# A two-layer cross-attention transformer on one core: the first cross group prepared eight groups ahead, extra rounds of maxima moved behind the second round of scores, constant rows written by DMA, and adjacent chunks for two copies

## The chip, the core and the metric

The kernel runs on one core of one Trainium2 chip. The time is device microseconds of one execution. Before the change three runs took 3248.24, 3252.8 and 3247.61 us; the median is 3248.24 us. Five engines work beside each other: TensorE (PE, with its weight loads PEld), VectorE (DVE), ScalarE (ACT), GpSimd (POOL) and SyncE (SP), which here only issues DMAs. Each engine runs its own instructions in the order in which the program has them, and waits on semaphores for the others.

## What is computed

Two layers, each with self attention, cross attention and a gated feed-forward, over 4 batches of 512 tokens with 320 features. Everything is float32. There are 20 heads of 16 features; self attention has 512 keys, cross attention 1601 keys from a context with 192 features.

```python
h1 = ln(x, n1_g, n1_b);  x = attn(h1, h1,      q1, k1, v1, o1_w, o1_b) + x
h2 = ln(x, n2_g, n2_b);  x = attn(h2, context, q2, k2, v2, o2_w, o2_b) + x
h3 = ln(x, n3_g, n3_b)
a, g = split(h3 @ ff_w1 + ff_b1);  x = (a * gelu(g)) @ ff_w2 + ff_b2 + x

def attn(x, ctx, wq, wk, wv, wo, bo):      # 20 heads of 16
    s = softmax((x @ wq) . (ctx @ wk) * 16 ** -0.5)   # over all keys
    return (s . (ctx @ wv)) @ wo + bo
```

## The kernel before, in words

**Groups.** Attention is cut into groups of 4 heads of one batch (`Unit`). A layer has 20 self groups (4 batches x 5 groups), then 20 cross groups, then 4 feed-forward units. I number the attention groups through: 0 to 19 are self groups of layer 0, 20 to 39 its cross groups, 40 to 59 the self groups of layer 1, 60 to 79 its cross groups. Group 20 and group 60 are the first cross group of a layer; the code calls them `early`.

**Maxima first.** The softmax subtracts a row's maximum inside the matmul: queries and keys lie in slots of 32 rows of which 16 are features and one is the negated maximum (in q) against a row of ones (in k). So before a group's scores can be made, its raw scores must be computed once in the other orientation (`max_pairs`, matmuls at L880 and L904 into PSUM tiles `sps`), reduced by VectorE (L896, L916), turned, and written into q by eight small DMAs on SP's queue (`max_end`, L951).

**Chunks and rounds.** `main` (L1042) walks over chunks of 128 keys: 4 chunks in a self group, 13 in a cross group. A chunk has two rounds. A round is two score matmuls (L1051, tiles `st`) and beside them, in the other half of TensorE's rows, a pair of maxima matmuls for a later group. ScalarE takes the exponential of each score tile into a `pr` tile (L1057). After the second round `flush` issues the product with the values of the chunk before (L1071, `av`); ScalarE copies it to a tile `vo` (L1087) and GpSimd adds that to the sum `o` (L1088). `pr` and `vo` share a ring of 8 buffers. Then `steps` takes work from queues (`chains`), each piece with a cost and a due round: projections of queries (L676), keys (L702, L732) and values (L807, L825), output projections (L998), transposed norms (L478).

**Extra rounds.** A self group's own rounds have room for exactly the maxima of the next self group (8 pairs), and a cross group's 26 rounds for the 26 pairs of the next cross group. The first cross group of a layer has no cross group in front of it, so its maxima need rounds of their own: four maxima matmuls at a time, two in one double PSUM tile (`ps_m`, 2 tiles of 2 banks) and two in single banks (`ps_st`, a ring of 4 that also holds scores, values and projections). `giver` decides when such a round is owed; in `main` it runs after `steps`, at L1112 to L1115, which means directly in front of the next chunk's two rounds.

**Preparing ahead.** While group i runs, the main loop (L1353) adds the projections of group i + 3, or of group i + 5 if that is `early`; `lead`, `add_norms` and `giver` have distances that go with it (4, 6 and 5 groups).

**Constant rows.** The key buffers `kbuf[1]` and `kbuf[2]` of cross attention hold ones and zeros outside of the features. `rows_of_ones` (L129) writes them on GpSimd: a memset and two passes over 64 partitions for each buffer of 128x1664. In layer 0 this is on a list `loads`, from which `main` takes one entry after each chunk; in layer 1 it follows the last feed-forward unit of layer 0, which uses the same buffers.

**Context keys and values.** Four 128-wide quarters go to four banks: two singles, which ScalarE copies out, and a double tile, which VectorE copies out (`quarter_banks`, L740 to L742, L832 to L837).

Of the kernel before, what the change touches and what calls it, by code (L numbers as in the profile page):

```python
# [22 lines left out]
P = 128  # L23
# [19 lines left out]
HALF = QT // 2  # L43
NHC = FF // P

PARTS = [(0, 2 * HG), (2 * HG, H)]
# [19 lines left out]
def kernel(ctx: ExitStack, tc: tile.TileContext, x, context, ws, out):  # L66
# [61 lines left out]

    def rows_of_ones(k, new=True):  # L129

        if new:
            nc.gpsimd.memset(k, 0.0)
        for b in range(2):
            rows = slice(b * GD, (b + 1) * GD)
            nc.gpsimd.tensor_scalar(k[rows], k[rows], zero[rows], ones[b][rows], ALU.mult, ALU.add)

# [6 lines left out]
    zero = const.tile([P, 1], F32, name="zero")  # L143
    nc.vector.memset(zero, 0.0)


# [449 lines left out]
    def lead(u):  # L596

        if u.i == 0:
            return 0
        return units[u.i - (4 if u.early else 2 if u.m == 0 else 1)].start  # L600

# [24 lines left out]
    def add_proj(u):  # L626
# [97 lines left out]
        def keys_of_context():  # L724
# [15 lines left out]
            for i, ps in enumerate(singles):  # L740
                nc.scalar.copy(stage[:, 2 * i, :], ps[:, : HALF + 32])
            nc.vector.tensor_copy(stage[:, 1::2, :], both[:, :, : HALF + 32])  # L742

# [42 lines left out]
    def quarter_banks(name):  # L786

        both = ps_m.tile([P, 2, 512], F32, tag="m", name=name)
        singles = [ps_st.tile([P, 512], F32, tag="st", name=name) for _ in range(2)]
        return [singles[0], both[:, 0], singles[1], both[:, 1]], singles, both  # L790

    def add_values(u):
# [24 lines left out]
        def values_of_context(i, s):  # L817
# [14 lines left out]
            for a, ps in enumerate(singles):  # L832
                nc.scalar.copy(vals[:, 4 * s + 2 * a, h0:h1, 0:DH], ps[:, :w].rearrange("p (h d) -> p h d", d=DH))
            nc.vector.tensor_copy(
                vals[:, 4 * s + 1 : 4 * s + 4 : 2, h0:h1, 0:DH],
                both[:, :, :w].rearrange("p a (h d) -> p a h d", d=DH),
# [205 lines left out]
    def main(u, give, nxt):  # L1042
# [49 lines left out]
        for c in range(u.nch):  # L1092
            extra = []
            if last:

                both = ps_m.tile([P, 2, N], F32, tag="m", name="st")
                round_of([lambda j=j: score(c, j, both[:, j % 2] if j > 1 else None) for j in range(HG)], [])
                tick()
            else:
                for odd in range(2):  # L1100
                    if odd:
                        tick()
                    pair, rounds = give(2 * c + odd)
                    extra += rounds
                    round_of([lambda j=j: score(c, j) for j in ((2, 3) if odd else (0, 1))], pair)
            u.scored = c + 1
            flush()
            late.append(lambda c=c: values(c))
            steps(None, 1 if extra or c == u.nch - 1 else 2)

            start["both"] = True
            for i, e in enumerate(extra):  # L1112
                if i and next_cost() is not None:
                    run(pick())
                round_of([], e)  # L1115
            start["both"] = False
            if not last and c == u.nch - 3:
                max_reduce(nxt)
                max_end(nxt)
            if loads:  # L1120
                loads.popleft()()
# [7 lines left out]
    def add_norms(i):  # L1129

        while norms and norms[0].i <= i + (1 if norms[0].kind == "ff" else 6):
            u = norms.popleft()
# [86 lines left out]

    EARLY = 9  # L1220

# [13 lines left out]
    def after(u):  # L1235

        stage[u.b] += 1
        if u.b == B - 1:
# [5 lines left out]
            if u.l + 1 < L:  # L1244
                if u.kind == "ff":
                    for k in kbuf[1:]:
                        rows_of_ones(k, False)
                    loads.extend(load_cross(u.l + 1))
# [17 lines left out]
    def giver(u):  # L1266

        ahead = []  # L1270
        for v in units[u.i + 1 : u.i + 6]:
            if v.kind == "ff":
                break
            if v.i <= u.i + 2 and (v.i == u.i + 1 or u.kind != "ff") or v.early:
                ahead.append(v)
# [5 lines left out]
        def give(h, alone=False):  # L1281
# [5 lines left out]
            most = 0.0  # L1287
            for v in ahead:
                total += left(v)
# [3 lines left out]
                if rest > 0:  # L1293
                    most = max(most, (total - rest * (not alone)) / (2 * rest))
                if left(v) and (rest == 1 or alone and rest < 1):
                    owed = max(owed, 1.0 if alone and rest > -4 else (left(v) + 1) // 2)
            owed += most * went if total else 0.0
            while owed >= 1.0 and any(left(v) for v in ahead) and not (alone and rounds and rest > -4):
                hand = [v for v in ahead if left(v) and all(v.pairs) and at_hand(v)]
                if not hand and ahead[0].start - 4 - clock["round"] > 1:  # L1300
                    break
                v = hand[0] if hand else next(v for v in ahead if left(v))
                at_once(v)
                rounds.append([f for q in v.pairs if q for f in q.popleft()])
# [34 lines left out]
    now(load_x(1))  # L1339
    rows_of_ones(kbuf[0][:, 4 * QT :])  # L1340
    loads.extend(load_x(2))
    for k in kbuf[1:]:
        loads.append(lambda k=k: rows_of_ones(k))
    for fs in (load_out(0, "o1_w"), load_x(3), load_cross(0), load_ff(0)):
# [8 lines left out]
    for i, u in enumerate(units):  # L1353
# [9 lines left out]
        start["both"] = u.kind == "ff"  # L1363
        for k in (3, 5):
            v = units[i + k] if i + k < len(units) else None
            if v is not None and v.kind != "ff" and v.early == (k == 5):
                add_proj(v)
# [30 lines left out]
```

## Time and profile before

| what | value |
|---|---|
| runs | 3248.24, 3252.8, 3247.61 us |
| profiled execution | 3249.95 us |
| its span, first to last instruction | 3248.2 us |
| TensorE clock granted, mean | 0.996 |
| DVE busy | 2061.2 us (63%) |
| ACT busy | 1969.5 us (61%) |
| POOL busy | 1217.6 us (37%) |
| self attention of layer 0 (scores of groups 0 to 19) | 33.8 to 429.7 us |
| cross attention and feed-forward of layer 0 | 429.7 to 1657.5 us |
| self attention of layer 1 | 1657.5 to 2045.4 us |
| cross attention and feed-forward of layer 1 | 2045.4 us to the end |

Busy shares say little here: four matmuls of 32 rows run beside each other, and a wait of 1 us between two rounds vanishes in a share of 98%. What can be read is the distance between the starts of successive rounds on TensorE, in the timeline: two rounds of one chunk stand 0.98 us apart, the second round and the `av` behind it 0.95 us, `av` takes 0.88 or 1.00 us. Where a distance is larger, TensorE waited, and the timeline's bracket behind an instruction names the wait. Every matmul of the program appears twice in the counts, as two passes.

### The profile page before, as it was taken

What the parts mean: (1) busy time and instruction counts of PE and PEld (TensorE: products, weight loads), DVE (VectorE), ACT (ScalarE), POOL (GpSimd) and SP (SyncE); (2) the same over time, 40 slices, a digit from 0 to 9 for tenths busy, and PEclk for the clock granted to TensorE, in tenths of its full rate; (3) what the DMA queues carried; (4) which work ended last, traced back from release to release, by engine and by line L of the source; (5) the groups of instructions that cost most, each with busy time, mean ns of one, the idle gap of its engine ahead of it and who ended that gap; (6) DMA issues with size and microseconds to landing.
All of it is one profiled execution on the core that took longest, in us unless ns stands there. A gap on an engine that the chain in (4) does not pass through costs nothing.

```text
span 3248.2 us, 81861 instructions
## 1 busy us (share of the span) xinstructions
PE 3197.9 (98%) x33970; PEld 1481.1 (46%) x33970; DVE 2061.2 (63%) x2663; ACT 1969.5 (61%) x3951; POOL 1217.6 (37%) x1627
## 2 busy tenths in 40 slices
PE   8999999999999999999999999999999999999999
PEld 3444444444444444354444444444444444443555
DVE  6777777777777777422247777777777777773221
ACT  3666567777777777611136665677778777775110
POOL 5545334434444443210234544344434444432000
PEclk9999999999999999999999999999999999999999
DMA  1121011100100100100002100010010010001000
GB/s 52 43 53 33 16 25 36 38 21 19 33 21 19 32 16 10 39 6 1 1 22 48 31 12 16 20 30 16 16 29 12 16 32 10 16 10 37 9 10 15
DMA packets 98008, 74.46 MB, mean 23 GB/s; under 512 B 42717, under 2 KB 88165, under 8 KB 97637
## 3 DMA queue, kind: packets, MB, share of 16 engines
q1 hardware_dynamic: 97552, 69.22, 8.8%
q8 instruction: 268, 4.39, 0.6%
q14 instruction: 104, 0.84, 0.1%
q0 software_dynamic: 64, 0.00, 0.0%
q10 hardware_dynamic: 20, 0.00, 0.0%
HBM read 33.04 MB, written 7.93 MB: 13 GB/s over the span
## 4 chain that ended last, share of the span: by engine, by line
PE 93%; DVE 2%; POOL 2%; issue 1%; ACT 1%; DMA 0%; SPq 0%; POOLq 0%; DVEq 0%
PE st L1051 25%; PE av L1071 20%; PE sps L880 14%; PE fps L1167 9%; PE yps L1206 5%; PE ops L998 3%; PE kps L732 3%; PE qps L676 3%; PE vps L825 3%; PE fps L1179 2%; PE vps L807 2%; PE sps L904 1%; PE kps L702 1%; PE hps L478 1%; DVE pm L896 1%
## 5 line engine op out<-in xcount | busy, mean ns | idle before, releaser
L1057 ACT ACTIVATE pr<-st 128x512 f32<-128x512 f32 (+1 forms) x2720 | 1414.4, 602 | 488.1 <-PE sps L880 343.0
L1051 PE MATMUL st<-q,kT 32*128 32x512 f32 (+1 forms) x5440 | 1382.9, 617 | 33.5 <-ACT pr L1057 12.9
L896 DVE TENSOR_REDUCE pm<-sps 128x2 f32<-128x1024 f32 (+1 forms) x970 | 1136.1, 1206 | 273.1 <-PE sps L880 265.5
L880 PE MATMUL sps<-kT,q 32*128 32x512 f32 x5120 | 1285.0, 623 | 2.3 <-DVE nmax L896 2.0
L1088 POOL TENSOR_TENSOR o<-o,vo 128x512 f32<-128x512 f32 x576 | 735.6, 1277 | 1392.1 <-ACT vo L1087 1220.0
L1051 PEld LDWEIGHTS st<-q,kT 32*128 32x128 f32 (+1 forms) x5440 | 516.0, 181 | 559.8 <-ACT pr L1057 313.2
L1071 PE MATMUL av<-pr,vals 128*32 128x512 f32 (+1 forms) x5440 | 732.7, 607 | 0.2
L896 DVE TENSOR_REDUCE nmax<-sps 128x2 f32<-128x1024 f32 (+1 forms) x343 | 378.8, 1145 | 156.7 <-PE sps L880 153.5
L880 PEld LDWEIGHTS sps<-kT,q 32*128 32x128 f32 x5120 | 408.6, 184 | 108.4 <-issue 87.0
L1087 ACT COPY vo<-av 128x512 f32<-128x512 f32 x576 | 348.0, 604 | 41.5 <-PE av L1071 38.7
L1071 PEld LDWEIGHTS av<-pr,vals 128*32 128x32 f32 (+1 forms) x5440 | 110.0, 108 | 498.5 <-ACT pr L1057 473.3
L1167 PE MATMUL fps<-hT,w 128*128 128x512 f32 x640 | 288.2, 599 | 1.1 <-DVE hid L1186 0.6
L1185 ACT ACTIVATE gl<-fps,b 128x512 f32<-128x512 f32 x80 | 50.6, 684 | 387.4 <-PE fps L1179 387.4
L624 POOL TENSOR_SCALAR q<-qst,keep,zero 64x128 f32<-64x128 f32 (+1 forms) x476 | 229.9, 483 | 49.7 <-ACT qst L688 16.7
L1167 PEld LDWEIGHTS fps<-hT,w 128*128 128x128 f32 x640 | 117.3, 190 | 148.6 <-issue 143.2
L1186 DVE SCALAR_TENSOR_TENSOR hid<-fps,b,gl 128x512 f32<-128x512 f32 x48 | 33.8, 746 | 163.1 <-ACT gl L1185 163.1
L998 PEld LDWEIGHTS ops<-wo,aT 112*32 112x32 f32 (+1 forms) x3072 | 98.2, 110 | 67.5 <-issue 36.3
L676 PE MATMUL qps<-hT,wq 112*32 112x128 f32 (+3 forms) x2880 | 125.5, 308 | 0.0
L998 PE MATMUL ops<-wo,aT 112*32 112x160 f32 (+1 forms) x3072 | 125.5, 299 | 0.0
L676 PEld LDWEIGHTS qps<-hT,wq 112*32 112x32 f32 (+1 forms) x2880 | 86.4, 110 | 79.2 <-issue 36.2
L426 POOL TENSOR_SCALAR root<-root 128x4 f32<-128x4 f32 x23 | 5.3, 231 | 301.3 <-DVE root L420 300.4
L491 POOL TENSOR_TENSOR x<-x,brow 128x320 f32<-128x320 f32 x96 | 83.5, 886 | 88.9 <-DVE hn L465 78.4
(88 smaller groups left out, 2194.6 us busy)
## 6 DMA issues: line engine op xcount, KB each, us to landing
kT<-kst SPq DMA_DIRECT2D x320, 48.0 KB
aT<-o SPq DMA_DIRECT2D x320, 32.0 KB
q<-turned SPq DMA_DIRECT2D x636, 1.0 KB
w<-in_L_xattn_ff_w_dram SPq DMA_DIRECT2D x20, 256.0 KB
ctxT<-ctxT SPq DMA_DIRECT2D x24, 208.0 KB
ctxT<-ctxT SPq DMA_DIRECT2D x12, 416.0 KB
ctxin<-in_ctx_dram SPq DMA_DIRECT2D x24, 192.0 KB
w<-in_L_xattn_ff_w_dram SPq DMA_DIRECT2D x20, 160.0 KB
```

The costliest lines, as they stand in the source:

```text
L624: nc.gpsimd.tensor_scalar(to, stage[rows, :w], keep[b][rows], more[rows], ALU.mult, ALU.add)
L676: nc.tensor.matmul(ps[to, :w], lhsT=wq[:n, k, gs], rhs=first.hT[:n, k, at[i] : at[i] + w], start=(k == 0), stop=(k == 2),)
L880: nc.tensor.matmul(ps, lhsT=u.q[j * SLOT : (j + 1) * SLOT, t * P : (t + 1) * P], rhs=u.kT[j * SLOT : (j + 1) * SLOT, u.k0 + s * 512 : u.k0 ...
L896: nc.vector.tensor_reduce(to[:, j : j + n], part, AX.X, ALU.max, negate=(ns == 1))
L998: nc.tensor.matmul(ps[f : f + m, : D // 2], lhsT=aT[:n, k, t * P + f : t * P + f + m], rhs=wo[:n, k, cols], start=(k == 0), stop=(k == 2),)
L1051: nc.tensor.matmul(st[:r, :], lhsT=u.kT[rows, u.k0 + u.cols[c] : u.k0 + u.cols[c] + r], rhs=u.q[rows, :], start=True, stop=True)
L1057: nc.scalar.activation(p[:r], st[:r], AF.Exp)
L1071: nc.tensor.matmul(ps[i * SLOT : (i + 1) * SLOT, :], lhsT=columns_of[:r, head : head + SLOT], rhs=pr.pop((c, j))[:r, :], start=True, stop= ...
L1087: nc.scalar.copy(vo, ps)
L1088: nc.gpsimd.tensor_tensor(u.o, u.o, vo, ALU.add)
L1167: nc.tensor.matmul(ps, lhsT=w1[:, k, i * FF + c * P : i * FF + (c + 1) * P], rhs=u.hT[:, k, :], start=(k == 0), stop=False,)
L1206: nc.tensor.matmul(ps[:, :D], lhsT=hid[c][:, t * P : (t + 1) * P], rhs=w2[:, c, :], start=(c == 0), stop=(c == NHC - 1),)
```

## The change

It has four parts.

1. **Distance.** A constant `AHEAD = 8` takes the place of 5 (and 4, 6 for the norm and its lead): the first cross group's norm, keys, queries and maxima are prepared from eight groups before it on. `EARLY`, which loads its context, goes from 9 to 7. `giver` looks at all coming groups up to the early one, counts those not yet prepared into the total that it spreads, and, in a self group, gives extra rounds to the early group unless another one is urgent.
2. **Place.** The first extra round of a chunk is issued directly behind the chunk's second round of scores, ahead of `flush` (the `av`) and `steps`; further extra rounds stay where they were.
3. **Constant rows.** One tile `blank` (128x128) is written by GpSimd once, at the start; `blanks(k)` copies it with DMAs on SP's queue to all column blocks of a key buffer, at most 5 blocks in one DMA: three DMAs for each large buffer, one for the small end of `kbuf[0]`. In layer 1 they go on the list `loads` too.
4. **Adjacent chunks.** Quarters 0 and 3 go to the single banks and 1 and 2 to the double tile (before: 0, 2 and 1, 3), so that VectorE's copy writes two adjacent quarters in place of every second one.

The diff, cut to its core:

```diff
+AHEAD = 8
...
-    def rows_of_ones(k, new=True):
-
-        if new:
-            nc.gpsimd.memset(k, 0.0)
-        for b in range(2):
-            rows = slice(b * GD, (b + 1) * GD)
-            nc.gpsimd.tensor_scalar(k[rows], k[rows], zero[rows], ones[b][rows], ALU.mult, ALU.add)
+    blank = const.tile([P, P], F32, name="blank")
+
+    def blanks(k):
+
+        n = k.shape[-1] // P
+        of = blank.rearrange("p (o w) -> p o w", o=1)
+        return [
+            lambda a=a, b=min(a + 5, n): dma(
+                out=k.rearrange("p (a w) -> p a w", w=P)[:, a:b], in_=of.to_broadcast([P, b - a, P])
+            )
+            for a in range(0, n, 5)
+        ]
...
+    nc.gpsimd.memset(blank, 0.0)
+    for b in range(2):
+        rows = slice(b * GD, (b + 1) * GD)
+        nc.gpsimd.tensor_scalar(blank[rows], blank[rows], zero[rows], ones[b][rows], ALU.mult, ALU.add)
...
-        return units[u.i - (4 if u.early else 2 if u.m == 0 else 1)].start
+        return units[u.i - (AHEAD - 1 if u.early else 2 if u.m == 0 else 1)].start
...
-                nc.scalar.copy(stage[:, 2 * i, :], ps[:, : HALF + 32])
-            nc.vector.tensor_copy(stage[:, 1::2, :], both[:, :, : HALF + 32])
+                nc.scalar.copy(stage[:, 3 * i, :], ps[:, : HALF + 32])
+            nc.vector.tensor_copy(stage[:, 1:3, :], both[:, :, : HALF + 32])
...
-        return [singles[0], both[:, 0], singles[1], both[:, 1]], singles, both
+        return [singles[0], both[:, 0], both[:, 1], singles[1]], singles, both
...
-                vals[:, 4 * s + 1 : 4 * s + 4 : 2, h0:h1, 0:DH],
+                vals[:, 4 * s + 1 : 4 * s + 3, h0:h1, 0:DH],
...
             u.scored = c + 1
+
+            start["both"] = True
+            if extra:
+                round_of([], extra[0])
+            start["both"] = False
             flush()
             late.append(lambda c=c: values(c))
             steps(None, 1 if extra or c == u.nch - 1 else 2)
-
-            start["both"] = True
-            for i, e in enumerate(extra):
+            for i, e in enumerate(extra[1:]):
                 if i and next_cost() is not None:
                     run(pick())
+                start["both"] = True
                 round_of([], e)
-            start["both"] = False
+                start["both"] = False
...
-        while norms and norms[0].i <= i + (1 if norms[0].kind == "ff" else 6):
+        while norms and norms[0].i <= i + (1 if norms[0].kind == "ff" else AHEAD + 1 if norms[0].early else 6):
...
-    EARLY = 9
+    EARLY = 7
...
                     for k in kbuf[1:]:
-                        rows_of_ones(k, False)
+                        loads.extend(blanks(k))
...
-        for v in units[u.i + 1 : u.i + 6]:
+        for v in units[u.i + 1 : u.i + AHEAD + 1]:
             if v.kind == "ff":
                 break
+            coming.append(v)
...
-            for v in ahead:
+            urgent = None
+            for v in coming:
+                if v not in ahead:
+                    total += v.steps
+                    continue
                 total += left(v)
...
                 if left(v) and (rest == 1 or alone and rest < 1):
+                    urgent = urgent or v
                     owed = max(owed, 1.0 if alone and rest > -4 else (left(v) + 1) // 2)
...
                 v = hand[0] if hand else next(v for v in ahead if left(v))
+                if u.kind == "self" and ahead[-1].early and urgent is None:
+
+                    v = ahead[-1]
+                    if v not in hand:
+                        break
...
-    rows_of_ones(kbuf[0][:, 4 * QT :])
+    now(blanks(kbuf[0][:, 4 * QT :]))
     loads.extend(load_x(2))
     for k in kbuf[1:]:
-        loads.append(lambda k=k: rows_of_ones(k))
+        loads.extend(blanks(k))
...
-        for k in (3, 5):
+        for k in (3, AHEAD):
             v = units[i + k] if i + k < len(units) else None
-            if v is not None and v.kind != "ff" and v.early == (k == 5):
+            if v is not None and v.kind != "ff" and v.early == (k == AHEAD):
```

More of the change, by code (lines that the diff above doesn't have):

```diff
@@ L832, in values_of_context @@
             for a, ps in enumerate(singles):
-                nc.scalar.copy(vals[:, 4 * s + 2 * a, h0:h1, 0:DH], ps[:, :w].rearrange("p (h d) -> p h d", d=DH))
+                nc.scalar.copy(vals[:, 4 * s + 3 * a, h0:h1, 0:DH], ps[:, :w].rearrange("p (h d) -> p h d", d=DH))
             nc.vector.tensor_copy(
-                vals[:, 4 * s + 1 : 4 * s + 4 : 2, h0:h1, 0:DH],
+                vals[:, 4 * s + 1 : 4 * s + 3, h0:h1, 0:DH],
                 both[:, :, :w].rearrange("p a (h d) -> p a h d", d=DH),
@@ L1266, in giver @@
     def giver(u):
-        ahead = []
-        for v in units[u.i + 1 : u.i + 6]:
+        ahead, coming = [], []
+        for v in units[u.i + 1 : u.i + AHEAD + 1]:
             if v.kind == "ff":
                 break
+            coming.append(v)
             if v.i <= u.i + 2 and (v.i == u.i + 1 or u.kind != "ff") or v.early:
```

## The prediction

> **What bounds the kernel now.** The page's first part says TensorE is busy for 3197.9 of 3248.2 us, and the chain of waits that ended last gives PE 93%. So a change that removes no matmul can only win where TensorE waits. Both programs, built but not run, have the same matmuls by kind and count; only their order differs, and it differs only at the start of layer 0 (group 0), the start of layer 1 (groups 40 to 42) and the end of both self stages (groups 10 to 19 and 50 to 59). I therefore read the timeline of those stretches and compared the distances between rounds with the undisturbed 0.98 us (round to round) and 0.95 us (round to `av`). There are two places of waiting.
>
> First, in group 1 of layer 0: the timeline of GpSimd, of ScalarE and of TensorE.
>
> ```profile
> 69.73 1.48 POOL L132 MEMSET kT<- 128x1664 f32 x1
> 71.32 3.57 POOL L135 TENSOR_SCALAR kT<-kT,zero,ones 64x1664 f32<-64x1664 f32 x2
> 74.95 1.54 POOL L132 MEMSET kT<- 128x1664 f32 x1
> 76.60 3.54 POOL L135 TENSOR_SCALAR kT<-kT,zero,ones 64x1664 f32<-64x1664 f32 x2
> 80.22 1.26 POOL L1088 TENSOR_TENSOR o<-o,vo 128x512 f32<-128x512 f32 x1
> ...
> 81.51 0.60 ACT L1057 ACTIVATE pr<-st 128x512 f32<-128x512 f32 x1 [9.31 <-POOL o L1088]
> ...
> 82.16 1.69 PE L1051 MATMUL st<-q,kT 32*128 32x512 f32 x2 [7.10 <-ACT pr L1057]
> ```
>
> The reader is to see one chain: GpSimd fills two key buffers from 69.73 to 80.14, the addition that frees a `vo` buffer stands behind them, the next exponential needs that buffer (it shares the ring of `pr`) and waits 9.31 us, and TensorE, out of score banks, waits 7.10 us.
>
> Second, every extra round of four maxima. TensorE and VectorE around one, in group 17:
>
> ```profile
> 373.25 1.61 PE L880 MATMUL sps<-kT,q 32*128 32x512 f32 x10
> ...
> 374.43 4.92 DVE L896 TENSOR_REDUCE nmax<-sps 128x2 f32<-128x1024 f32 x5 [0.33 <-PE sps L880]
> ...
> 376.30 1.29 PE L1051 MATMUL st<-q,kT 32*128 32x512 f32 x3 [1.01 <-DVE nmax L896]
> ```
>
> The extra round starts at 373.25, the next chunk's rounds at 374.23 and 376.30, its `av` at 377.97: distances of 2.07 and 1.67 where 0.98 and 0.95 are usual, 1.8 us lost, 1.9 with 0.1 at the extra round itself. The reason is in the middle line: five reductions in a row, 4.92 us, which is the pair of 1.22, two single banks of 0.68, and two pairs of the following rounds. The second round needs the banks of the singles, and those are reduced last. Seven such rounds stand in each layer's groups 16 to 18 (one, three, three). Group 19 waits 0.5 us once and, with four maxima and the sixteen small ones of the last 65 keys in one place, another 2.6 us. Together 7 x 1.9 + 3.1 = 16.5 us a layer.
>
> The clock is the third view, busy time by stage:
>
> ```profile
> core 0: us, PE busy (x) PEld busy (x) DVE busy (x) ACT busy (x) POOL busy (x), PEclk, DMA share, GB/s
> ...
> 84.00:86.00 2.00, 2.00 (x16) 0.77 (x12) 1.19 (x1) 1.09 (x2) 1.75 (x4) 0.65 0.00 0
> ...
> 408.30:429.70 21.40, 19.77 (x202) 8.54 (x194) 18.26 (x26) 10.86 (x22) 5.88 (x10) 0.92 0.04 7
> 2025.60:2045.40 19.80, 18.17 (x200) 8.51 (x192) 16.96 (x25) 10.73 (x22) 6.05 (x10) 1.00 0.03 7
> ```
>
> Groups 19 and 59 do the same work; the one at clock 0.92 takes 1.6 us more.
>
> **The change, part by part.**
>
> *Constant rows.* GpSimd loses 1.48 + 3.57 + 1.54 + 3.54 us in group 1. Without them its root chain ends at 69.8, the `vo` of 69.66 is added by 71.5, and the exponential runs when its predecessors end, at 72.2. TensorE's next round then comes at 73.58 + 1.41 (the keys projection in front) = 75.0 in place of 82.16: 7.2 us. The two rounds at 82.16 and 84.51 run at half clock, 1.8 us, and a later exponential waits 0.9 us for the same backlog, 0.8 us of it seen on TensorE. Sum 9.8 us. What is late next is the maximum row of group 2: SP issues its eight DMAs from 67.97 to 72.35, and one takes 2.6 to 3.2 us to land (the view of that line, L951), so the last lands at about 74.9, with no slack against 75.0. I take 9.3. The second fill, 7.15 us at 1656.39 in layer 1, gains nothing: the first addition after it comes at 1678.57.
>
> The DMAs in its place: 640 or 384 pieces of 512 B. The trace has no such transfer from SBUF to SBUF; between 0 and, from the ring's mean of 47 ns per packet (8.8% of 16 engines' span over 97,552 packets) on 16 engines, 640 x 47 / 16 = 1.9 us, plus 0.6 us of SP for each, as a `kT` issue takes. They go one per chunk, and other loads follow six chunks later than before: the output weights move from about group 1 to group 2 or 3 against their first use in group 6, the cross weights to about group 8 against group 12. Cost 0. The new `blank` costs GpSimd about what the fill of `kbuf[0]`'s end cost (0.2 + 2 x 0.45 us), earlier, beside the first loads.
>
> *Place of the extra round.* Now: round (double bank A), round (B), extra (A, singles 0 and 1), `av` (single 2), steps (single 3 and on), next rounds. From the start of the first round: its pair is reduced from +1.26 to +2.44 (the group 17 chunk at 362.98), so the extra round waits from +1.93 to +2.46, 0.5 us. VectorE reduces the second pair until +3.6, the extra pair until +4.85, the singles until +5.5 and +6.2. `av` begins at +3.4 and ends at +4.3. With one values piece (0.77) the next round wants its banks at +5.1 and has them at +5.5 and +6.2: 0.9 us. So 1.4 us for that layout; 0.5 where query and key projections (2.7 us) stand between; 0.8 with 24 output projections; 1.5 and 1.7 with nothing between, twice in a row; 1.8 and 1.0 where four context banks or 24 query matmuls follow. The bounds for one are 0 and the 1.9 of today; the layouts average 1.2, and I use those.
>
> *Distance.* The after program has one extra round in group 14, two in 15, one in 16, two in 17, two in 18 and the small ones in 19: eight and the tail, as before, over six groups in place of four. By the layouts 1.4, 1.4 + 0.5, 0.8, 1.5 + 1.7, 1.8 + 1.0, 0.5 = 10.6 us a layer against 16.5. In layer 1 today's group 59 waits 1.6 less, so the gains are 5.9 and 4.3. Moved with it: keys of the first cross group from group 15 to 12, norm and queries from 16 to 13. The keys' twelve slot DMAs occupy SP for 12 x 0.61 us, three per chunk; the maximum row of group 18 is issued by 375.0 and lands near 377.6, needed at 380.76, so 1.8 us of them in front fits. On GpSimd four additions of the bias row (3.3 us), eight and four query slots (4.2 + 2.5) and the root chain (3.6) move to groups 12 and 13, and the queries of two groups now stand together in front of one `o` addition. A root chain in front of `o` costs 2.4 to 4 us in groups 5, 10, 45 and 50 (group 5: exponential waits 2.88) and 0.6 in group 15, where keys and values are beside it. The moved chain is behind one addition and beside keys and output projections, so the near row is group 15. Between -0.5 and +2.5 net; I take 0.5 lost per layer. Gain 5.4 + 3.8.
>
> *Starts.* Groups 0 and 40 are bound by VectorE: the same reductions, with gaps of 0.56 and 0.79 us in group 0 and 1.0, 0.8 and 0.5 us in group 40 before the extra rounds, which a round issued earlier can fill. Group 42 has one extra round, 1.9 to 1.4. I take 1 and 2 us.
>
> *Adjacent chunks.* 88 VectorE copies (0.42 to 0.62 us) of the same size; TensorE's waits on them are not among the listed ones. 0.
>
> [...] For the half clock in group 19 I see no idle stretch over about 1 us in front of it. [...] I count it as gone, and 1.7 us more or less in the range.
>
> **Sum.** 9.3 + 1 + 5.4 + 2 + 3.8 = 21.5 us. The profiled execution took 3249.95 us, 1.7 us around its span; 3249.95 - 21.5 = 3228.4. The median of the runs lies 1.7 below that execution, so the median after is **3227 us**.
>
> **Rivals.**
>
> *The waits at extra rounds only move.* VectorE's 2.6 us per extra round stays, and in group 17 its sum (8 pairs 9.8, two extra 5.2, the finish of a group 2.3, output adds 0.6: 17.9 us) exceeds TensorE's 15 us. Then the stage gains nothing, the moved GpSimd work costs 1 us a layer, and 9.3 + 1 - 2 = 8.3 remain: 3240. For it: the waits end at VectorE. Against: in groups 8, 9 and 12 to 15 VectorE is busy 80.7 of 104.7 us, so that the groups over which the rounds are spread have 4 us to spare each.
>
> *VectorE hides nearly all of it.* Waits fall to 0.5 per extra round, 4.5 a layer: 12 + 10.4 + 9.3 + 3 = 34.7, 3214.
>
> *The start doesn't give its 9 us.* If the maximum row or another load is late in group 2 and the stage gains nothing, about 3244.
>
> *Slower: the block copies hold up the maximum rows.* They share SP's queue and the rings with the eight DMAs of L951, which have no slack in groups 1 to 3. Six groups' rows are concerned. To lose the 21.5 us and 6.5 more, each copy must delay a row by (21.5 + 6.5) / 6 = 4.7 us, more than twice the 1.9 us worked out above; if the copies ran on a single engine (640 x 47 ns = 30 us) it would be far slower, 3270. Against: the destination spans 128 partitions as the weight loads do, which reach 246 GB/s in slices of the DMA view from 60 to 110 us.
>
> **How the numbers follow.** Forecast 0.56 (its own range 3219 to 3235), waits only move 0.25, nearly all hidden 0.09, the start fails 0.06, slower 0.04. The range from 3213 to 3240 leaves out the last two and part of the second. A measurement here can tell 0.2%, 6.5 us, from no change, that is below 3241.7 or above 3254.7: faster 0.90, same 0.06, slower 0.04.
>
> **What would show it.** The line of 9.31 us on ScalarE is gone and group 2 starts about 9 us earlier. In groups 14 to 18 an extra round starts about 2.5 us after its chunk's first round and the next round comes 0 to 1 us late, not 2; groups 12 to 19 together shrink from 165.7 us (264.0 to 429.7) by about 5. Group 13's exponentials wait for `o` at most 1 us. I am wrong if ScalarE shows new waits on GpSimd in groups 12 to 14, if rounds in groups 1 to 3 or 40 to 42 wait for `q<-turned`, or if half clock appears in groups 14 to 18.

## The result and the profile after

The changed kernel takes 3215.27 us (median of 4 runs, 3212.79 to 3217.71) against 3250.31 us before (4 runs, 3247.61 to 3252.8): a ratio of 0.9892, with a 95% interval of 0.9875 to 0.9909. That is 35 us less, where 21.5 were forecast and 3227 us was the time on record. The profiled execution took 3212.79 us, its span 3211.0 us, 37.2 us shorter than the span before. TensorE is busy for 3170.7 us (3197.9 before), VectorE for 2062.9, ScalarE for 1966.1, GpSimd for 1203.1 us.

The spans, cut at the starts of groups on TensorE (us):

| stage | before | after | difference | forecast | length at half clock, before and after |
|---|---|---|---|---|---|
| start, groups 0 to 2 | 103.4 | 92.0 | -11.4 | -10.3 | 13.7, 0 |
| groups 3 to 11 | 160.6 | 162.4 | +1.8 | 0 | 3.4, 6.8 |
| groups 12 to 19 | 165.7 | 161.8 | -3.9 | -5.4 | 3.4, 0 |
| groups 20 to 39 and feed-forward | 1227.9 | 1219.7 | -8.2 | 0 | 0, 0 |
| groups 40 to 42 | 62.6 | 62.3 | -0.3 | -2 | 0, 0 |
| groups 43 to 51 | 161.6 | 158.5 | -3.1 | 0 | 6.8, 0 |
| groups 52 to 59 | 163.7 | 161.8 | -1.9 | -3.8 | 0, 0 |
| groups 60 to 79 and the rest | 1202.8 | 1192.6 | -10.2 | 0 | 0, 0 |

In a stretch at half clock the granted clock is 0.50 (134.31 to 137.72 us of the profile after), and a score matmul takes 1.06 us in it (at 135.71) and 0.59 behind it (at 139.17). From this I estimate that such a stretch costs half its length where TensorE has work throughout, and less elsewhere. So the two rows with +1.8 and -3.1, in which the program is nearly unchanged, are the clock: 1.7 more and 3.4 less. The large surprise is the cross groups, 18.4 us in two stages for which nothing was forecast.

**The start.** The timeline of the changed kernel in group 1:

```profile
67.48 0.20 POOL L443 TENSOR_TENSOR root<-root,root 128x4 f32<-128x4 f32 x1
68.19 1.27 POOL L1099 TENSOR_TENSOR o<-o,vo 128x512 f32<-128x512 f32 x1 [0.51 <-ACT vo L1098]
...
70.26 1.34 SPq L138 DMA_DIRECT2D kT<-blank  x2
...
71.18 1.28 POOL L1099 TENSOR_TENSOR o<-o,vo 128x512 f32<-128x512 f32 x1 [1.71 <-ACT vo L1098]
...
72.86 0.70 PE L1062 MATMUL st<-q,kT 32*128 32x512 f32 x2
...
74.02 2.07 ACT L1068 ACTIVATE pr<-st 128x512 f32<-128x512 f32 x4 [0.65 <-PE sps L891]
```

Where two fills stood between the root chain and the addition, the addition now follows within 0.5 us, and GpSimd itself waits for ScalarE. The exponential that waited 9.31 us for `o` waits 0.65 us for the scores. Group 2 starts at 72.86 where it started at 82.16. The block copies (L138) go out two at a time on SP's queue, and no round of TensorE in groups 1 to 3 waits for them or for the maximum row.

**An extra round.** TensorE and VectorE around two extra rounds in group 17:

```profile
364.73 0.70 PE L1062 MATMUL st<-q,kT 32*128 32x512 f32 x2
...
365.99 2.36 DVE L907 TENSOR_REDUCE nmax<-sps 128x2 f32<-128x1024 f32 x2
...
367.27 1.14 PE L891 MATMUL sps<-kT,q 32*128 32x512 f32 x8 [0.40 <-DVE nmax L907]
368.34 1.06 PE L1082 MATMUL av<-pr,vals 128*32 128x512 f32 x8
368.44 2.42 DVE L907 TENSOR_REDUCE pm<-sps 128x2 f32<-128x1024 f32 x3
...
371.29 0.59 PE L1062 MATMUL st<-q,kT 32*128 32x512 f32 x2
...
373.65 1.14 PE L891 MATMUL sps<-kT,q 32*128 32x512 f32 x8 [1.34 <-DVE nmax L907]
```

The chunk's first round starts at 364.73 and the extra one 2.54 us later (2.5 was forecast). VectorE then reduces the extra pair and the singles from 368.44 to 370.86, so the next chunk's second round comes at 371.29 instead of 370.31, 1.0 late. But the chunk after it also has an extra round, and that one starts 2.36 us behind its second round where 0.95 is undisturbed.

**The clock**, as in the view of busy time by stage. The columns after the stretch and its length are busy time of PE, PEld, DVE, ACT and POOL with their instructions, the granted clock, the DMA share and GB/s:

```profile
core 0: us, PE busy (x) PEld busy (x) DVE busy (x) ACT busy (x) POOL busy (x), PEclk, DMA share, GB/s
400.50:416.20 15.70, 15.21 (x194) 7.18 (x190) 12.22 (x19) 10.43 (x23) 6.54 (x11) 1.00 0.03 5
2002.80:2018.40 15.60, 15.12 (x192) 7.12 (x188) 12.14 (x19) 10.35 (x23) 6.52 (x11) 1.00 0.03 5
...
130.50:134.00 3.50, 2.24 (x31) 0.97 (x23) 1.48 (x2) 0.67 (x2) 2.39 (x7) 1.00 0.36 104
134.20:137.70 3.50, 3.50 (x18) 1.41 (x21) 1.76 (x4) 1.59 (x5) 0.00 (x0) 0.52 0.02 6
1736.00:1739.50 3.50, 2.25 (x31) 0.98 (x23) 1.49 (x2) 0.70 (x2) 2.36 (x7) 1.00 0.43 3
1739.50:1743.00 3.50, 3.50 (x26) 1.48 (x30) 2.94 (x7) 3.12 (x7) 0.00 (x0) 1.00 0.01 1
```

Groups 19 and 59 (first two rows) now both run at full clock and take equally long. The last four rows are two places with the same work and the same wait, in groups 5 and 45: behind the one TensorE falls to 0.52 for 3.4 us, behind the other not.

### The profile page after: what moved, and what is told of

The parts are those of the page before. It is cut to its first block, busy times and chain, and to the rows that moved or that the text cites. A ratio compares the mean times of both kernels' runs of the same rounds, so it can differ in the third digit from the quotient of the medians.

```text
span 3211.0 us, 81827 instructions
## 1 busy us (share of the span) xinstructions
PE 3170.7 (99%) x33970; PEld 1465.7 (46%) x33970; DVE 2062.9 (64%) x2663; ACT 1966.1 (61%) x3951; POOL 1203.1 (37%) x1617
## 4 chain that ended last, share of the span: by engine, by line
PE 63%; DVE 2%; POOL 1%; ACT 0%; issue 0%; DMA 0%; SPq 0%; POOLq 0%; DVEq 0%
PE st L1062 15%; PE av L1082 13%; PE fps L1182 9%; PE sps L891 8%; PE yps L1221 5%; PE fps L1194 2%; PE ops L1009 2%; PE kps L743 2%; PE qps L687 2%; PE vps L836 2%; PE sps L915 1%; PE vps L818 1%; PE kps L713 1%; PE hps L489 1%; DVE nmax L907 1%; DVE pm L907 1%
## 5 line engine op out<-in xcount | busy, mean ns | idle before, releaser
L635 POOL TENSOR_SCALAR q<-qst,keep,zero 64x128 f32<-64x128 f32 (+1 forms) x476 | 230.4, 484 | 48.6 <-ACT qst L699 15.4
```

The lines of the kernel that those rows point to most:

```text
L635: nc.gpsimd.tensor_scalar(to, stage[rows, :w], keep[b][rows], more[rows], ALU.mult, ALU.add)
```

## Where the cross groups' 18 us come from

The list of waits (engine and line, waited for, us in total, times, longest) changes most in one line. Before:

```profile
DVE vals L834 <- ACT vals L833: 86.4, 48, 2.5
...
PEld sps L880 <- DVE vals L834: 4.8, 16, 0.3
```

After (the code stands eleven lines lower):

```profile
DVE vals L845 <- PE vps L836: 63.3, 46, 2.0
```

One of the 48 places, on the timeline, before:

```profile
508.12 0.54 ACT L833 COPY vals<-vps 128x192 f32<-128x192 f32 x2 [1.47 <-PE vps L825]
...
508.69 0.56 DVE L834 COPY vals<-vps 128x384 f32<-128x384 f32 x1 [2.13 <-ACT vals L833]
508.79 1.04 PE L1051 MATMUL st<-q,kT 32*128 32x512 f32 x4
...
509.16 2.54 DVE L896 TENSOR_REDUCE pm<-sps 128x2 f32<-128x1024 f32 x2
509.30 0.30 PEld L880 LDWEIGHTS sps<-kT,q 32*128 32x128 f32 x4 [0.30 <-DVE vals L834]
...
510.36 1.07 PE L1071 MATMUL av<-pr,vals 128*32 128x512 f32 x8
```

and after:

```profile
495.44 0.54 ACT L844 COPY vals<-vps 128x192 f32<-128x192 f32 x2 [1.47 <-PE vps L836]
495.50 0.56 DVE L845 COPY vals<-vps 128x384 f32<-128x384 f32 x1 [1.62 <-PE vps L836]
...
496.11 0.59 PE L1062 MATMUL st<-q,kT 32*128 32x512 f32 x1
...
496.40 2.36 DVE L907 TENSOR_REDUCE pm<-sps 128x2 f32<-128x1024 f32 x2 [0.34 <-PE sps L891]
...
497.17 1.07 PE L1082 MATMUL av<-pr,vals 128*32 128x512 f32 x8
```

VectorE's copy takes 0.56 us both times. Before, it starts when both of ScalarE's copies are done (508.69); after, it runs beside them (495.50 against 495.44). Before, it ends at 509.25, and the second round's maxima, which need the same double bank, are loaded at 509.30. The round that starts at 508.79 is followed by `av` 1.57 us later. After the change that distance is 1.06 us. VectorE also has an idle 0.34 us in front of the reduction where before it came straight from the copy. 48 such places and 18.4 us make 0.38 us each.

Before, VectorE wrote quarters 1 and 3 in one strided instruction, and between them lies quarter 2, which ScalarE writes. No byte was shared, yet in all 48 places the copy starts 0.03 us after ScalarE's second copy ends. With adjacent quarters the wait listed is for TensorE in 46 places and for ScalarE in none. That the reach across quarter 2 makes the program wait fits e1 to e3 below, but it isn't the whole rule: the keys' copy had the same order of quarters before and never waited for ScalarE. Its line in the list of before:

```profile
DVE kst L742 <- PE kps L732: 62.8, 40, 2.4
```

In all 40 places it starts 0.3 to 0.4 us before ScalarE's second copy ends. It writes each quarter of its tile whole, the values' copy only the columns of 8 or 12 of the 20 heads; whether this is the difference isn't shown.

## The experiments

| kernel | median (range), us | ratio to before, 95% | start | self ends | cross | lost to half clock |
|---|---|---|---|---|---|---|
| before | 3250.31 (3247.61 to 3252.8) | | 103.4 | 329.4 | 2430.7 | 13.7 |
| after | 3215.27 (3212.79 to 3217.71) | 0.9892 [0.9875, 0.9909] | 92.0 | 323.6 | 2412.3 | 3.4 |
| e1, values' quarters as before | 3234.69 (3233.61 to 3235.89) | 0.9951 [0.9939, 0.9964] | 94.3 | 323.6 | 2430.2 | 8.5 |
| e2, the same, copied one by one | 3225.82 (3222.02 to 3226.4) | 0.992 [0.9907, 0.9934] | 94.5 | 324.0 | 2420.4 | 10.2 |
| e3, before with adjacent chunks | 3233.11 (3230.34 to 3233.34) | 0.9944 [0.9932, 0.9957] | 103.8 | 327.4 | 2414.6 | 13.7 |
| e4, large fills on GpSimd | 3225.81 (3222.09 to 3228.03) | 0.9923 [0.991, 0.9935] | 101.4 | 323.6 | 2414.2 | 10.2 |
| e5, place as before | 3222.1 (3221.31 to 3222.28) | 0.9917 [0.9903, 0.993] | 94.9 | 327.6 | 2415.7 | 8.5 |
| e6, distance as before | 3213.53 (3213.04 to 3213.77) | 0.989 [0.9877, 0.9904] | 93.4 | 322.8 | 2412.7 | 5.1 |
| e7, both as before | 3218.76 (3218.3 to 3219.41) | 0.9907 [0.9893, 0.992] | 94.4 | 325.6 | 2413.2 | 10.2 |
| e8, singles first | 3206.77 (3206.45 to 3213.17) | 0.9875 [0.9861, 0.9888] | 93.7 | 321.0 | 2414.1 | 13.7 |
| e9, root chain on VectorE | 3232.56 (3232.13 to 3239.21) | 0.9955 [0.9943, 0.9968] | 92.2 | 328.0 | 2433.7 | 11.9 |
| e10, e9 and e8 together | 3229.05 (3224.92 to 3230.37) | 0.9933 [0.992, 0.9947] | 94.2 | 326.1 | 2433.3 | 17.1 |
| e11, e8 and e9 for self norms only | 3203.44 (3202.52 to 3204.17) | 0.9859 [0.9842, 0.9875] | 91.4 | 319.0 | 2415.5 | 3.4 |

The last four columns are of one profiled execution each: groups 0 to 2, groups 12 to 19 and 52 to 59 together, groups 20 to 39 and 60 to the end together, and half the length of all stretches at half clock before TensorE's last matmul. That of e8 is its slowest run of the four. Each ratio is to runs of the kernel before made beside that kernel (medians 3248.76 to 3250.31 us), so small differences between kernels are safer in the ratios than in the times.

### Adjacent chunks, undone and alone (e1, e2, e3)

```diff
# e1, in the changed kernel
+            pss = [pss[0], pss[1], pss[3], pss[2]]
...
-                nc.scalar.copy(vals[:, 4 * s + 3 * a, h0:h1, 0:DH], ...)
+                nc.scalar.copy(vals[:, 4 * s + 2 * a, h0:h1, 0:DH], ...)
...
-                vals[:, 4 * s + 1 : 4 * s + 3, h0:h1, 0:DH],
+                vals[:, 4 * s + 1 : 4 * s + 4 : 2, h0:h1, 0:DH],
```

> The changed kernel with one part undone: the values' quarters 0, 2 and 1, 3 again, keys as changed. Theory A (VectorE's copy of every second quarter waits for ScalarE's two copies, because its write lies between theirs; with adjacent quarters it waits for TensorE alone, and the double bank is free earlier): the 18 us that the cross groups won come back, 3232 to 3235 us, and VectorE's copies wait for ScalarE some 86 us in all. Theory B (the cross groups won by something else: less half clock, other order): 3213 to 3218.

```diff
# e2: as e1, but
+            for a in range(2):
+                nc.vector.tensor_copy(vals[:, 4 * s + 1 + 2 * a, h0:h1, 0:DH], ...)
```

> As the run before, but VectorE copies its two quarters one at a time, so that neither write spans one of ScalarE's. Theory A: the wait for ScalarE is gone although the quarters are not adjacent; the second copy costs some 0.2 to 0.3 us of VectorE in 48 places, so 3215 to 3224. Theory C (it is the access pattern of the strided copy, or the order of the banks): as the run before, 3232 to 3235.

e3 has the adjacent quarters, of keys and values, in the kernel before, and nothing else.

> The kernel before with the adjacent quarters alone, for keys and values. Theory A: 17 to 19 us less than before, 3231 to 3234. Theory B: within 3 us of before.

e1, in which the keys stay as changed, gives back 19.4 us, and its cross groups take 2430.2 us, as those before (2430.7): the whole gain is that of the values' copy. e3 wins 16.7 us against its own runs of before (3249.86); by the profiles 16.1 us of it in the cross groups and 2.0 at the self ends. The list of waits of e1 has the old line again:

```profile
DVE vals L846 <- ACT vals L845: 84.4, 46, 2.5
```

and that of e2, whose quarters are as far apart as those of e1 but copied singly, has not:

```profile
DVE vals L847 <- PE vps L837: 65.3, 46, 2.0
```

So the wait for ScalarE costs the time, not the place of the data; and the strided write itself is no slower, 0.49 us in e1 and in the changed kernel. e2 wins 8.9 us of e1's loss back, ends 2 us above the 3215 to 3224 expected, and stays 10.6 above the changed kernel. Its two copies take 0.64 us together where one takes 0.49, which is 7.1 us over 48 places, and its cross groups take 8.1 us longer than those of the changed kernel (1.7 of them half clock). But the two copies overlap: from the start of the first to the end of the second it is 0.55 us, 3 us more over all places. So the second copy explains a part of what e2 still loses, and the rest stays open.

### The constant rows back on GpSimd (e4)

```diff
-        loads.extend(blanks(k))
+        loads.append(lambda k=k: rows_of_ones(k))
```

> The changed kernel with the two large key buffers filled on GpSimd again in both layers, all else as changed. My theory of the start (the fill stands in front of the addition that frees a vo buffer): ScalarE waits about 9 us for o in group 1, and the time is 8 to 11 us more than the changed kernel, 3223 to 3227. Rival (the 11.4 us won in groups 0 to 2 come from the place of the extra rounds): within 3 us of the changed kernel.

e4 loses 10.5 us, and its start takes 101.4 us where the changed kernel has 92.0. The idle stretch of 7.1 us on TensorE is there again (from 72.6), with half clock behind it (10.2 us lost so in the whole profile, 3.4 in that of the changed kernel). This part is confirmed by itself: it is worth some 10 us and acts in group 1. The start of layer 1 takes 62.3 us with either fill.

### Place and distance (e5, e6, e7)

```diff
# e5: the place
-            start["both"] = True
-            if extra:
-                round_of([], extra[0])
-            start["both"] = False
...
-            for i, e in enumerate(extra[1:]):
+            for i, e in enumerate(extra):
# e6: the distance
-AHEAD = 8
+AHEAD = 5
...
-    EARLY = 7
+    EARLY = 9
# e7: both
```

> The changed kernel with the extra rounds behind the steps again, directly in front of the next chunk; distance of eight groups kept. My theory (the place shortens the wait of an extra round from 1.9 to about 1.3 us, whatever the distance): groups 12 to 19 and 52 to 59 take about 4 us more each than in the changed kernel, 3220 to 3226 us. Rival (spreading over more groups alone ends the waits, the place does nothing): 3213 to 3218.

> The changed kernel with AHEAD = 5 and EARLY = 9, the extra rounds behind the second round as changed. If the distance carries the gain of the self stages, groups 12 to 19 take as long as before, 3217 to 3223 us; if the place carries it and the GpSimd work that the distance moves to groups 12 to 14 costs 1 to 2 us a layer, it is as fast as the changed kernel or faster, 3211 to 3217.

> The changed kernel with distance and place both as before; constant rows and adjacent quarters as changed. The sum of the other two parts alone: 3250 less 11 for the start and less 17 to 18 for the cross groups, 3219 to 3224 us.

Neither e6 nor e7 is quite the order of before: the rewritten `giver` stays in both. It puts three extra rounds in group 17, four in group 18 and the rest in group 19, where the kernel before has one, three and three in groups 16 to 18.

*Distance.* With the new place, the old distance is as fast as the new one (e6 lies within the range of the changed kernel), although the extra rounds stand in fewer groups. With the old place the new distance loses 3.3 us (e5 against e7). So the eight groups are worth nothing here.

*Place.* It wins 5.2 us by the medians with a distance of five (e7 to e6) and 6.8 with eight (e5 to after). Of each, 5.1 us are half clock in the profiled executions (10.2 against 5.1, and 8.5 against 3.4). Without half clock the self ends are about 1.1 us shorter with five (2.8 less 1.7) and 4.0 us with eight, 2.0 each where 4 were expected. All runs of e7 have a mean clock of 0.997 and all of e6 0.998, so it may be the place that brings the half clock; no run here shows it.

*Both.* As made, the two edits are worth 3.5 us by the medians (e7, just under the 3219 us expected, against after). e7's profile is 5.5 us longer than that of after and loses 6.8 more to half clock, so that no gain outside of it is shown.

*`giver`.* e7's self ends take 325.6 us, 1.7 of it half clock; those of e3, with distance, place and `giver` as before, 327.4 without any. The fill does not touch them (323.6 us in e4 and in after). The difference of 3.5 us is an estimate of what the rewritten `giver` wins. No run here has it alone.

### The order inside an extra round (e8)

VectorE's middle row in group 17 above reduces the double tile first and the two single banks behind it, while the next rounds' scores ask for the single banks. e8 issues the singles first:

```diff
-                rounds.append([f for q in v.pairs if q for f in q.popleft()])
+                rounds.append([f for q in reversed(v.pairs) if q for f in q.popleft()])
```

> The changed kernel, and in an extra round the heads 0 and 1, which go to single banks, ahead of the heads 2 and 3, which go to the double one. In the changed kernel TensorE waits 0.6 us for the double bank and the next round waits for the singles, which VectorE reduces last. With the singles first, TensorE can begin the extra round at once and the singles are free 1.2 us earlier: 0.5 to 0.9 us less for each of 20 such rounds, 3200 to 3208 us. Rival (VectorE's sum of work sets the time of these groups, not the order in it): 3213 to 3218.

8.5 us less than the changed kernel. Each end of the self stages is 1.3 us shorter although each has a stretch at half clock (3.4 us long, so 1.7 us) that the changed kernel has not. The start of layer 1 takes 60.4 instead of 62.3 us. The timeline of the same chunks, from the reductions of the extra round on:

```profile
367.18 2.41 DVE L907 TENSOR_REDUCE pm<-sps 128x1 f32<-128x512 f32 x3
...
368.25 0.70 PE L1062 MATMUL st<-q,kT 32*128 32x512 f32 x2
...
369.22 0.59 PE L1062 MATMUL st<-q,kT 32*128 32x512 f32 x2
...
372.56 1.45 PE L891 MATMUL sps<-kT,q 32*128 32x512 f32 x4 [0.90 <-DVE nmax L907]
```

VectorE now takes the single banks (128x512) first, and the next chunk's second round comes 0.97 us after its first, where it was 1.96. The extra round behind it still waits for VectorE. So the order of release mattered here, at no cost.

### The root chain off GpSimd (e9, e10, e11)

The largest waits left in the self groups are four of this kind (timeline, group 5 of the changed kernel):

```profile
131.88 0.20 POOL L443 TENSOR_TENSOR root<-root,root 128x4 f32<-128x4 f32 x1
132.03 1.26 POOL L1099 TENSOR_TENSOR o<-o,vo 128x512 f32<-128x512 f32 x1
133.33 0.60 ACT L1068 ACTIVATE pr<-st 128x512 f32<-128x512 f32 x1 [2.91 <-POOL o L1099]
```

Thirteen operations on 128x4 numbers (3.5 us) hold up an addition, and with it ScalarE. e9 puts them on VectorE:

```diff
-        eng = nc.vector if start["on"] else nc.gpsimd
+        eng = nc.vector
```

> The changed kernel with the inverse root's chain of thirteen small operations on VectorE throughout, nothing else. Measured: in the profile of the changed kernel this chain, 3.5 us on GpSimd, stands in front of the addition to o at 132.03, 223.26, 1737.51 and 1827.08 us (groups 5, 10, 45, 50), and ScalarE's next exponential waits 2.91, 2.51, 2.90 and 2.89 us for that addition; the two half-clock stretches of 3.4 us (134.3 and 226.5) begin right behind two of them. Theory (the chain on GpSimd is on the path there): the four waits go, some 9 of 11.2 us, since VectorE needs 2.2 us for the chain and has some slack, and with them up to 1.7 us each of two to four half-clock stretches: 3201 to 3207 against 3215.3, no half clock at 134 and 226. Rival (VectorE is as near the path as GpSimd, and its chain delays the copies and reductions by as much): 3212 to 3220, with new waits for VectorE in these four groups.

> The previous kernel with heads 0 and 1 first in the extra rounds, that is with their single banks reduced before the double tile. This order alone gave 3206.8 (3206.5 to 3213.2), 8.5 us less than the changed kernel, of which the stages' tables explain about 8: 1.3 in each end of the self stages beside a half-clock stretch of 1.7 in each, 1.9 at the start of layer 1. If the two edits act in different places (theory) their gains add: 3193 to 3199. If part of the gain of the order was half clock that happened to fall elsewhere (rival), it is 3198 to 3204, and the stages 12 to 19 and 52 to 59 are no shorter than 160.5 us.

Both expectations failed: e9 is 17.3 us slower than the changed kernel, outside the rival's range too, and e10 22.3 slower than e8. By groups, 5, 10, 45 and 50 do become shorter (2.4, 2.4, 0.8, 0.8 us), and no half clock follows them. But group 12 and 52 are 2.2 longer each, and 22, 23, 27, 32, 62 and 67 together 21.9; 11.9 of this is half clock in groups 22, 27, 32 and 62. (Group 23 has no chain of its own; it follows 22.) The timeline of e9 in group 22:

```profile
546.66 1.26 POOL L1099 TENSOR_TENSOR o<-o,vo 128x512 f32<-128x512 f32 x1 [1.65 <-ACT vo L1098]
546.67 1.28 DVE L442 TENSOR_SCALAR root<-root 128x4 f32<-128x4 f32 x1
...
548.86 1.22 DVE L907 TENSOR_REDUCE pm<-sps 128x2 f32<-128x1024 f32 x1
...
550.13 1.76 PE L915 MATMUL sps<-kT,q 32*128 32x65 f32 x14 [2.61 <-DVE pm L907]
```

The chain runs on VectorE from 544.16 to 548.94 in one piece, and the pair of maxima that TensorE's banks wait for stands behind it. Its first three operations were VectorE's before too; the thirteen added take 3.6 us, not the 2.2 expected, since an operation of 0.17 us took 1.28 (546.67) beside GpSimd's addition (546.66, 1.26 us). TensorE waits 2.61 us, a half-clock stretch of 6.8 us begins at 549.4 (score matmuls take 1.06 us in it, at 552.86), and the next round comes 5.51 us after its predecessor.

e11 keeps VectorE's chain only where groups became shorter:

```diff
-    def inverse_root(var):
+    def inverse_root(var, own=False):
...
-        eng = nc.vector if start["on"] else nc.gpsimd
+        eng = nc.vector if own or start["on"] else nc.gpsimd
...
-            s["rstd"] = inverse_root(s["mv"][:, :, 1])
+            s["rstd"] = inverse_root(s["mv"][:, :, 1], i == 0)
```

> Heads 0 and 1 first in the extra rounds, and the inverse root's chain on VectorE for the norms of self attention only; the norms of cross attention and feed-forward keep it on GpSimd. With every chain on VectorE (3232.6), groups 5, 10, 45 and 50 became 2.4, 2.4, 0.8 and 0.8 us shorter, but groups 12 and 52 (the first cross group's norm) 2.2 longer each and groups 22, 23, 27, 32, 62 and 67 together 21.9 longer, because there the chain stands in front of a pair of maxima and is itself held up beside GpSimd's additions. Theory (place decides, not the engine): the gains of groups 5, 10, 45 and 50 remain, 6.4 us, and the losses go: 3197 to 3203 against 3206.8 of the order alone. Rival (the trade is even: what half clock leaves one place appears at another): 3203 to 3209.

3203.44 us: the fastest of the kernels here, 11.8 us below the changed kernel, yet 3.3 below e8 where 4 to 10 were expected. The 6.4 us counted for it held the loss by half clock of two of the four groups; without that the groups gain 0.7 to 0.8 us each, 3.0 together, though each exponential had waited 2.5 to 2.9. The larger gains in its own profile (2.4 us in three of the groups) are against the one run of e8 with half clock in those places, so the rival was nearer here: the plain gain is small, and what the clock adds depends on the execution (a mean of 0.996 in e8's slowest run, 0.998 in its three others).

## Why the prediction came out as it did

The time after lies in the range, near its lower end, and the direction was right, but the sum was right in one part of three. That it came this near is in part luck: a part put at nothing won half of the result, and another won less than was forecast.

- **Constant rows**, 9.3 and 1 us forecast for the start: confirmed. The chain was read rightly, and undoing it alone costs 10.5 us. The start's -11.4 in the table holds some 2 us of chance: of the kernels with block copies, those with a stretch at half clock near 49 us spend 93.4 to 94.9 us there, those without 91.4 to 92.2, and the profiled execution of before had it. The maximum row of group 2 and the block copies held up nothing.
- **Place of the extra round**, right in its mechanism: an extra round about 2.5 us after its chunk's first, the next round 1 us late, no longer 2. In cost it was somewhat low: summed over the distances between rounds, the waits at extra rounds in groups 14 to 19 are about 13.3 us where 10.6 were forecast and 16.5 stood before. Two terms carry that: two extra rounds in successive chunks of group 17 cost 1.7 and 2.5 us where 1.5 and 1.7 were taken, and the first of group 16 cost 1.85 where 0.8 was taken. VectorE has no idle stretch between those of group 17 (none listed from 362.24 to 377.25 us).
- **Distance**, forecast to spread the rounds at 0.5 us of loss a layer for the moved GpSimd work: the spreading gained nothing (e6). The moved work brought one new wait, at the start of group 14 and again in layer 1: `295.85 0.38 ACT L699 ACTIVATE qst<-qps 128x256 f32<-128x256 f32 x1 [2.47 <-POOL q L635]`. ScalarE's copy of queries waits for GpSimd, where an addition to `o` and slot copies stand in a row, and the next `av` comes 1.2 us late. A new wait of ScalarE on GpSimd in groups 12 to 14 was named as a sign of being wrong, and for this part it was one. In layer 1's start 2 us were forecast and 0.3 came. Place and distance with their starts were put at 11.2 us (5.4 + 3.8 + 2); the stages show 6.1, of which 1.7 is half clock in group 19, and the estimate above gives most of the rest to the rewritten `giver`, which the forecast did not count by itself.
- **Adjacent chunks**: the step that failed, the one that put a term at nothing. "88 VectorE copies (0.42 to 0.62 us) of the same size; TensorE's waits on them are not among the listed ones. 0." It is worth 17 to 19 us, half of the whole result. The copies are of the same size indeed. What the change removed was not work but a wait in front of them, and that wait was in the list of before, 86.4 us of it. I looked for TensorE as the one waiting, and for places where the order of instructions differs. An order compared engine by engine does not show that an instruction waits for one engine fewer. VectorE's idle time looked harmless because VectorE was busy only 63% of the span; here it stood between the double bank and the next round's maxima. Of the TensorE waits there was even a small line, 4.8 us for 16, below those I read.
- **The clock**: 1.7 us of group 19 ((1 - 0.92) x 21.4 us) were counted as gone, and groups 19 and 59 are both at 1.00. That the waits there brought the half clock isn't shown by this: in group 45 a stretch begins behind a wait of 1.23 us before (1761.34) and none behind one of 1.25 us after (1739.45).

One rival's sum was off: if the start gave nothing, 10.3 us less would have been won, which makes 3237 and not 3244.

The parts undone in turn, 10.5 (e4), 19.4 (e1) and 3.5 (e7), add up to 33.4 of 35.0 us, and the rewritten `giver`, which none of them undoes, is not among them: half clock moves each of these by some microseconds (10.2, 8.5 and 10.2 us are lost to it in these profiles, 3.4 in that of the changed kernel). The rival that VectorE hides nearly all of the extra rounds came closest in time (3214) and was wrong in mechanism, and the rival in which the waits at extra rounds only move is nearer to what they did.

## What to carry to other kernels

When two engines fill one tile, give each a contiguous part, or look up whether the one waits for the other: a strided write can be made to wait for a writer of the part between (the values' copy was, 86.4 us in 48 places before; the keys' wasn't, in 40), and with the next round's maxima behind it that cost 19.4 us in all (e1). Before a part of a change is put at nothing, look up its line in the list of waits as the one who waits, and follow what is behind it on its engine, however idle that engine is on average. When small work is moved to an engine with slack, ask for each place separately what stands behind it: the same chain gained 6.4 us in four groups and lost 26.3 behind seven others (e9).

## What the hardware showed beyond that

**Half clock on a grid.** In the profiles of before and after the stretches at half clock (granted 0.50) are 3.41 or 6.83 us long (but for the last of a span), and within one profile their starts lie on a grid of 3.413 us, to within 0.01 us. Before, they are 47.85, 78.57, 146.84, 423.31, 1761.34 and 1853.50, which is 0, 9, 29, 110, 502 and 529 steps from the first; after, 134.31 and 226.47 are 27 steps apart. Except behind the fills (7.10 us), the last idle stretch of TensorE that began in front of them was 0.58 (group 19 before) to 1.26 us (group 5 after); in e9's group 22 it was 2.61 us. The same wait brought half clock in one group and not in another, or in one execution and not in another: before, 1.23 us in groups 5, 45 and 50 was followed by it and 1.23 us in group 10 (236.42) not; after, 1.26 us in group 5 and 0.87 in group 10 were, 1.25 us in groups 45 and 50 not. What decides isn't shown. In the profiled executions between 3.4 and 17.1 us are lost so, which is why two profiles alone can't be compared to a few microseconds.

**Small VectorE operations beside GpSimd's.** In e9, nine operations of the inverse root that began during an addition of GpSimd (1.26 us) took 0.9 to 1.3 us instead of 0.16 to 0.17 and ended within 0.03 us of it; one in such a place took 0.17. Two of the nine stand in group 22: 1.28 us from 546.67, with the addition from 546.66, and 0.88 us from 544.16, with one from 543.74. In the changed kernel seven operations of 128x4 began during an addition, took 0.23 to 1.20 us (the longest at 782.06, with the addition from 781.97) and ended 0.03 us after it. Of the operations beside GpSimd's slot copies there (0.55 to 0.58 us), some took 0.17 us and the longest 0.42 (57.85).
